# Two decoder layers on one core: ranks of eight experts on VectorE alone, and the order of the work made anew

## The chip, the cores and the metric

The kernel runs on one core of a Trainium2 chip. The metric is the device time in microseconds; lower is better. The core's engines work through queues of their own, each strictly in the order of the program: TensorE (PE, matmuls), VectorE (DVE), ScalarE (ACT), GpSimd (POOL), and SyncE (SP), which issues most transfers.

## The reference, cut to what matters

Sixteen sequences of 128 tokens with 256 features pass through two layers. Layer 0: causal attention, attention over a context with 16 heads, and a feed-forward net in which each token uses 4 of 16 blocks. Layer 1: self-attention, attention over the context in windows, and a mixture of eight experts:

```python
scores = jax.nn.sigmoid(x @ gate_weight.T)              # (tokens, 8)
topk_w, topk_idx = jax.lax.top_k(scores, 2)
topk_w = topk_w / (topk_w.sum(-1, keepdims=True) + 1e-20) * 2.5
combine = jnp.einsum('tk,tke->te', topk_w, jax.nn.one_hot(topk_idx, 8))
y = jnp.einsum('tei,ehi->teh', silu(g) * u, w_down)     # g, u: x by each expert's weights
out = jnp.einsum('te,teh->th', combine, y) + shared_out # an expert that all tokens use
```

Every step is preceded by a normalisation and added to its input. `top_k` breaks ties in favour of the lower index. The kernel gets the two largest by ranks: the rank of an expert is the number of experts with a larger score, plus the number of those with an equal score that come before it.

## The kernel before

The work is cut into eight lanes of two sequences (256 tokens). A lane's state `x0` to `x7` stays on chip from the first load to the last store. A lane is a chain of short steps that changes engine at almost every one: matmuls into one of four PSUM banks, copied or scaled by ScalarE or VectorE, sums and masks on VectorE, products and powers on GpSimd. One lane alone would leave TensorE idle most of the time, so several are interleaved.

The interleaving is made by a planner, the class `Turns`, while the program is being written out. Each step of a lane is a generator that yields the engine that it wants next, and the buffers that it takes (`yield DVE, dict(rank=2)`). `run` (line 229) picks, among all threads that wait, the one that can start first by the planner's own clock, and of equals the one with the lower rank; `charge` moves that clock. The order in which the steps are picked is the order of the instructions in every engine's queue, and nothing changes it later. The clock has constants: `PART` (added to TensorE at each turn, line 262), `RELEASE` (added to the time at which a buffer comes free, line 118), and in `indexed` (line 162) the time until an indirect transfer has landed.

`TURN` (line 1424) lists in which order the lanes begin layer 0 and layer 1; at most five are in flight. At the end of layer 1 the lanes part. Lanes 0 to 4 form a group: `routing` (line 954) ranks the experts and writes each token into a table sorted by expert; when all five are there, `plan` and 27 times `expert_tile` (line 1093) fetch one expert's weights and 128 tokens by two indirect transfers on GpSimd's queue, compute (`xgt`, `gu2`, `hT2`, `y2` on TensorE), and write the result `yo` back; `combining` (line 1145) then fetches four rows of results for each token of a lane, again by indirect transfers (`yg`), adds them to `x`, and stores it. `shared` (line 1011) is the expert that all tokens use. Lanes 5 to 7 run `expert_ffn` (line 1249) instead: all eight experts for every token, with weights that are zero for those not chosen. There a router's logits (`rt`) become scores (`sc`), the scores ranks, the ranks shares (`sel`), which are split into three parts of bfloat16 (`chosen`) and transposed by TensorE (`ptt`) before the experts' outputs can be weighted (`wb`).

`ranks` (line 636) is called for the 16 blocks of layer 0 (8 times) and for the eight experts of layer 1 (8 times). It makes two tensors of all pairs: `eq`, where another's score is equal, and `gt`, where it is larger. GpSimd multiplies `eq` by a triangle of ones and adds it to `gt`; VectorE sums over the others.

Of the kernel before, what the change touches and what calls it, by code (L numbers as in the profile page):

```python
# [9 lines left out]
F32 = mybir.dt.float32  # L10
I32 = mybir.dt.int32
BF16 = mybir.dt.bfloat16
U8 = mybir.dt.uint8
AF = mybir.ActivationFunctionType
ALU = mybir.AluOpType
AX = mybir.AxisListType

B, S, D = 16, 128, 256
P = 128
DC = D // P  # L20
G = 2
NL = B // G
# [9 lines left out]
NE, TOPE = 8, 2  # L32
# [42 lines left out]
PE, DVE, ACT, POOL, SP = "PE", "DVE", "ACT", "POOL", "SP"  # L75
# [6 lines left out]
class Turns:  # L82
# [7 lines left out]
    HOP = 70.0  # L90
    HOP_FROM_PE = 200.0
    SWITCH = 91.0
    PART = 0.0
    RELEASE = 0.0

    def __init__(self, nc, limits):
        self.nc = nc
# [64 lines left out]
    def indexed(self, out, out_index, src, src_index):  # L162

        at = lambda i: None if i is None else bass.IndirectOffsetOnAxis(ap=i, axis=0)
        self.charge(POOL, 1050.0)
        self.moved(4 * int(np.prod((src if src_index is None else out).shape)))
        self.now.at += 2000.0
        self.nc.gpsimd.indirect_dma_start(out, at(out_index), src, at(src_index))  # L168

    def fetch(self, out, src):  # L170
# [102 lines left out]
def decoder(ctx: ExitStack, tc: tile.TileContext, a: dict, out: bass.AP):  # L273
# [5 lines left out]
    small = ctx.enter_context(tc.tile_pool(name="small", bufs=4))  # L279
# [46 lines left out]
    def along(t, n):  # L326

        return t.unsqueeze(2).to_broadcast([t.shape[0], t.shape[1], n])
# [28 lines left out]
    class Sorted:  # L357
# [27 lines left out]
        rank=2, selT=2, p0=3, pT0=3, unseen=4, chosen=3, swap=1, words=1, top=3,  # L385
    )
    q = Turns(nc, LIMITS)

    def new(tag, shape, name, dtype=F32):
        return work.tile(shape, dtype, tag=tag, name=name, bufs=LIMITS[tag])  # L390
# [245 lines left out]
    def ranks(scores, n, tri_at):  # L636

        tri = consts[:, tri_at : tri_at + n * n].rearrange("p (e f) -> p e f", f=n)
        shape = [P, G, n, n]
        other = scores.unsqueeze(2).to_broadcast(shape)  # L640
        own = scores.unsqueeze(3).to_broadcast(shape)
        yield DVE, dict(rank=2)
        gt = new("rank", shape, "gt", BF16)
        eq = new("rank", shape, "eq", BF16)
        q.dve("tensor_tensor", eq, other, own, ALU.is_equal)
        q.dve("tensor_tensor", gt, other, own, ALU.is_gt)
        yield POOL
        q.pool("tensor_tensor", eq, eq, tri.unsqueeze(1).to_broadcast(shape), ALU.mult)
        q.pool("tensor_tensor", gt, gt, eq, ALU.add)
        yield DVE  # L650
        rank = small.tile([P, G, n], F32, tag=f"rank{n}", name="rank")
        q.dve("tensor_reduce", rank, gt, AX.X, ALU.add)
        q.give("rank", 2)
        return rank
# [594 lines left out]
    def expert_ffn(l):  # L1249
# [10 lines left out]
        rank = yield from ranks(sc, NE, C_TRI8)  # L1260
        sel = small.tile([P, G, NE], F32, tag="sel", name="sel")
        q.dve("scalar_tensor_tensor", sel, rank, float(TOPE), sc, ALU.is_lt, ALU.mult)
        den = small.tile([P, G], F32, tag="den", name="den")
        q.dve("tensor_reduce", den, sel, AX.X, ALU.add)
        q.dve("tensor_scalar", den, den, 1e-20, None, ALU.add)
        q.dve("reciprocal", den, den)
        q.dve("tensor_tensor", sel, sel, along(den, NE), ALU.mult)
        q.dve("tensor_scalar", sel, sel, 2.5, None, ALU.mult)
        yield DVE, dict(chosen=1)

        share = chosen.pop(0)
# [137 lines left out]
    def layer_1(l):  # L1409
        yield from self_attention(l)  # L1410
        yield from windowed_attention(l)
        ended.append((1, l))
        g = group_of.get(l)
        if g is not None:
            yield from routing(l)
            g.left -= 1
            at = q.now.at
            q.start(shared(l), 2 * NL + l + NL, at)
            if g.left == 0:
                q.start(sorted_experts(g), 2 * NL + min(g.lanes), at)  # L1420

    IN_FLIGHT = 5

    TURN = [(0, l) for l in range(6)]
    for l in range(NL):
        TURN += [(1, l), (0, l + 6)] if l + 6 < NL else [(1, l)]

    def more():
        n = begun[0]
# [119 lines left out]
```

## Time and profile before

| | |
|---|---|
| median of three timed runs | 829.65 us (828.49 to 832.1) |
| the profiled execution: own time | 827.16 us |
| its span, first to last instruction | 825.4 us |
| mean granted clock of TensorE | 0.985 |
| busy: PE, DVE, ACT, POOL | 777.8, 478.4, 393.0, 450.4 us |
| POOL, product eq<-eq and sum gt<-gt for eight experts | 488 and 425 ns, 8 times each |
| DVE, eq<-sc and gt<-sc | 291 and 284 ns, 8 times each |
| DVE, sum rank<-gt over 128 and over 512 elements | 278 and 676 ns, 8 times each |

A row of the profile names the line of the source, the engine, the operation, output and input tiles, their size in partitions by elements, how many instructions there were, and how long they took. Nearly all compute instructions have the line of a helper of `Turns` (L135 and L140 for TensorE, L144 VectorE, L149 ScalarE, L155 GpSimd, L168 indirect transfers), so the names of the tiles tell the steps apart. In rows in order of time the first two numbers are the start in us from the span's start and the time taken; the bracket at the end is how long the engine was idle before, and what it waited for. A matmul in float32 is two records. The 40 digits of a row of slices are tenths of busy time, or of full clock, in stretches of 20.6 us.

### The profile page before, as it was taken

The page shows a single profiled execution, that of the slowest core. Times are in us where ns is not written, and L with a number is a line of the kernel's source. Part 1 is how long each engine was busy: PE and PEld are TensorE (multiplying, and loading weights), DVE is VectorE, ACT ScalarE, POOL GpSimd, SP SyncE. Part 2 cuts the span into 40 slices and gives each one's busy share as a digit, 9 for nine tenths or more (in the row PEclk, how much of TensorE's full clock was granted, in tenths as well). Part 3 has the DMA queues.
Part 4 walks back from the last instruction along what each step waited for, and adds up shares of the span by engine and source line. Part 5 has one row for each costly group of instructions (what it writes and reads, how often), then busy time and mean ns, then how long its engine had stood idle before and what let it go on. Part 6 is the DMA issues. An engine that isn't in the chain of part 4 may idle for free.

```text
span 825.4 us, 19793 instructions
## 1 busy us (share of the span) xinstructions
PE 777.8 (94%) x7886; PEld 617.3 (75%) x7886; DVE 478.4 (58%) x1257; ACT 393.0 (48%) x874; POOL 450.4 (55%) x720
## 2 busy tenths in 40 slices
PE   6999999999999999999999999998997799999998
PEld 5777678878778777877777777776665677787776
DVE  4455736545735536746675668567765654434464
ACT  4546345343355364745663666575446244443300
POOL 5325535514335356656876747776675664654071
PEclk9999999999999999999999999999998899999999
DMA  8457540601201002020003301111110534455042
GB/s 292 154 155 217 147 141 25 185 17 36 58 2 40 14 30 62 2 65 15 15 20 100 126 27 39 63 56 40 50 56 15 178 94 133 153 185 160 26 133 84
DMA packets 60940, 70.41 MB, mean 85 GB/s; under 512 B 8848, under 2 KB 52496, under 8 KB 60208
## 3 DMA queue, kind: packets, MB, share of 16 engines
q1 hardware_dynamic: 51584, 46.20, 17.9%
q0 software_dynamic: 5376, 19.40, 7.7%
q10 hardware_dynamic: 3888, 3.54, 1.2%
q8 instruction: 62, 1.02, 0.5%
q14 instruction: 30, 0.25, 0.1%
HBM read 43.96 MB, written 20.97 MB: 79 GB/s over the span
## 4 chain that ended last, share of the span: by engine, by line
PE 77%; DVE 7%; POOL 6%; ACT 4%; issue 3%; DMA 1%; ACTq 0%; DVEq 0%; POOLq 0%
PE s L135 15%; PE pj L135 11%; PE y L135 11%; PE gu L135 10%; PE pr L135 9%; PE hp L135 8%; PE oT L135 4%; PE tps L140 3%; PE o L140 2%; ACT p L149 2%; DVE top L144 2%; POOL rstd L155 2%; PE rt L135 1%; POOL we L168 1%; POOL qs L155 1%
## 5 line engine op out<-in xcount | busy, mean ns | idle before, releaser
L144 DVE TENSOR_REDUCE top<-s 128x8 f32<-128x1024 f32 x96 | 113.0, 1218 | 53.7 <-PE s L135 50.0
L149 ACT ACTIVATE p<-s 128x1024 f32<-128x1024 f32 x96 | 95.1, 1024 | 63.1 <-PE s L135 61.6
L155 POOL TENSOR_TENSOR qs<-qT,less 128x512 f32<-128x512 f32 x48 | 61.8, 1293 | 66.2 <-ACT less L149 56.4
L135 PE MATMUL s<-qs,kb 32*128 32x128 f32 x1536 | 62.1, 288 | 7.3 <-POOL qs L155 3.1
L135 PEld LDWEIGHTS s<-qs,kb 32*128 32x128 f32 x1536 | 51.6, 189 | 22.6 <-issue 6.7
L155 POOL TENSOR_SCALAR rstd<-mv 128x2 f32<-128x2 f32 x77 | 18.5, 241 | 91.5 <-DVE mv L144 80.3
L135 PE MATMUL hp<-srcT,L_w 128*128 128x256 f32 x256 | 66.0, 387 | 0.0
L135 PE MATMUL s<-kb,qT 32*128 32x256 f32 x768 | 61.4, 405 | 4.3 <-DVE top L144 4.2
L149 ACT ACTIVATE sg<-gu 128x256 f32<-128x256 f32 (+1 forms) x67 | 22.9, 342 | 80.6 <-PE gu L135 78.7
L135 PE MATMUL y<-L_w,hm 128*128 128x256 f32 x256 | 58.8, 383 | 0.7 <-ACT gained L149 0.6
L155 POOL TENSOR_TENSOR rstd<-rstd,power 128x2 f32<-128x2 f32 x77 | 55.3, 718 | 6.4
L155 POOL TENSOR_SCALAR kb<-kT,consts 128x256 f32<-128x256 f32 x96 | 53.5, 568 | 6.9 <-ACT kT L149 6.0
L149 ACT ACTIVATE hm<-hp,cols 128x256 f32<-128x256 f32 x64 | 26.9, 471 | 59.1 <-PE hp L135 58.8
L135 PEld LDWEIGHTS s<-kb,qT 32*128 32x128 f32 x768 | 38.2, 184 | 21.2 <-issue 8.5
L135 PEld LDWEIGHTS y<-L_w,hm 128*128 128x128 f32 x256 | 47.7, 190 | 8.4 <-issue 1.1
L135 PE MATMUL oT<-p,v 128*32 128x128 f32 x1536 | 52.6, 278 | 0.8 <-ACT gained L149 0.5
L135 PEld LDWEIGHTS hp<-srcT,L_w 128*128 128x128 f32 x256 | 44.3, 190 | 11.6 <-issue 2.6
L144 DVE SCALAR_TENSOR_TENSOR sg<-sg,gu 128x256 f32<-128x256 f32 (+1 forms) x67 | 24.4, 364 | 43.6 <-ACT sg L149 43.3
L135 PE MATMUL gu<-srcT,gu 128*128 128x256 f32 x192 | 48.0, 399 | 1.3 <-DVE hm L144 0.7
L140 PE MATMUL tps<-consts,xn 128*128 128x128 f32 x244 | 38.4, 282 | 10.3 <-DVE xn L144 7.2
L135 PEld LDWEIGHTS oT<-p,v 128*32 128x32 f32 x1536 | 39.6, 111 | 11.0 <-issue 7.5
L168 POOL DMA_INDIRECT we<-in_L_experts,tile_weights x27 | 26.0, 965 | 39.6 <-PE hT L140 18.8
(211 smaller groups left out, 1796.7 us busy)
## 6 DMA issues: line engine op xcount, KB each, us to landing
to_experts<-zero SPq DMA_DIRECT2D x7, 1280.0 KB, 5.8
unseen<-hidden SPq DMA_DIRECT2D x128, 64.0 KB, 2.6
c<-in_ctx SPq DMA_DIRECT2D x16, 256.0 KB, 4.7
by_experts<-yo ACTq DMA_DIRECT2D x27, 128.0 KB, 1.9
x<-in_x SPq DMA_DIRECT2D x8, 256.0 KB, 6.6
L_w<-in_L_w SPq DMA_DIRECT2D x2, 1024.0 KB, 5.6
hidden<-plain SPq DMA_DIRECT2D x32, 64.0 KB, 1.6
swap<-kT SPq DMA_DIRECT2D x16, 128.0 KB, 2.0
```

Of the source, the lines that this page charges most:

```text
L135: self.nc.tensor.matmul(out, lhsT, rhs, **kw)
L140: self.nc.tensor.transpose(out, src, ident)
L144: getattr(self.nc.vector, name)(out, *args, **kw)
L149: getattr(self.nc.scalar, name)(out, *args, **kw)
L155: getattr(self.nc.gpsimd, name)(out, *args, **kw)
L168: self.nc.gpsimd.indirect_dma_start(out, at(out_index), src, at(src_index))
```

## The change

`ranks` has a branch of its own for the eight experts. One tensor holds both comparisons side by side, `equal` and `above`; the product with the triangle is made by VectorE in place, and one sum over both axes gives the ranks. GpSimd has no part in it any more, and the branch takes one buffer of the kind `rank` instead of two. In `expert_ffn` the shares are divided and scaled by 2.5 in one operation instead of two. The rest alters the planner: `PART` and `RELEASE` are 20 and 30 instead of 0, an indirect transfer is taken to land 1000 ns later, the shared expert of a lane has rank 16 + l instead of 24 + l, and seven lanes begin layer 0 before the first begins layer 1, instead of six. With these the planner picks another order for the whole program.

```diff
-    PART = 0.0
-    RELEASE = 0.0
+    PART = 20.0
+    RELEASE = 30.0
...
-        self.now.at += 2000.0
+        self.now.at += 3000.0
         self.nc.gpsimd.indirect_dma_start(out, at(out_index), src, at(src_index))
...
         other = scores.unsqueeze(2).to_broadcast(shape)
         own = scores.unsqueeze(3).to_broadcast(shape)
+        if n == NE:
+
+            yield DVE, dict(rank=1)
+            t = new("rank", [P, G, n, 2, n], "above", BF16)
+            above, equal = t[:, :, :, 0, :], t[:, :, :, 1, :]
+            q.dve("tensor_tensor", equal, other, own, ALU.is_equal)
+            q.dve("tensor_tensor", above, other, own, ALU.is_gt)
+            q.dve("tensor_tensor", equal, equal, tri.unsqueeze(1).to_broadcast(shape), ALU.mult)
+            rank = small.tile([P, G, n], F32, tag=f"rank{n}", name="rank")
+            q.dve("tensor_reduce", rank, t, AX.XY, ALU.add)
+            q.give("rank")
+            return rank
...
-        q.dve("tensor_tensor", sel, sel, along(den, NE), ALU.mult)
-        q.dve("tensor_scalar", sel, sel, 2.5, None, ALU.mult)
+        q.dve("scalar_tensor_tensor", sel, sel, 2.5, along(den, NE), ALU.mult, ALU.mult)
...
-            q.start(shared(l), 2 * NL + l + NL, at)
+            q.start(shared(l), 2 * NL + l, at)
...
-    TURN = [(0, l) for l in range(6)]
+    TURN = [(0, l) for l in range(7)]
     for l in range(NL):
-        TURN += [(1, l), (0, l + 6)] if l + 6 < NL else [(1, l)]
+        TURN += [(1, l), (0, l + 7)] if l + 7 < NL else [(1, l)]
```

## The prediction

> **What bounds the kernel now.** I read the engines' shares first, then the 40 slices, then the list of waits for TensorE alone, then the stretches of 25 us, and last the instructions in order of time at the places that these pointed to.
>
> ```profile
> PE 777.8 (94%) x7886; PEld 617.3 (75%) x7886; DVE 478.4 (58%) x1257; ACT 393.0 (48%) x874; POOL 450.4 (55%) x720
> PE   6999999999999999999999999998997799999998
> PEclk9999999999999999999999999999998899999999
> ```
>
> TensorE (PE) is busy 777.8 of 825.4 us, so 47.6 us idle. The slices are full until the 29th; the losses lie at the start, and from about 560 us on. By stretches the late ones look like this (columns: PE busy, weight loads, DVE, ACT, POOL, then the granted clock, the DMA share, GB/s):
>
> ```profile
> 600.00:625.00 25.00, 22.07 (x347) 15.61 (x344) 17.61 (x55) 12.05 (x24) 17.57 (x29) 0.93 0.14 39
> 625.00:650.00 25.00, 21.10 (x191) 17.38 (x192) 13.29 (x52) 15.00 (x30) 13.74 (x26) 0.86 0.22 70
> 650.00:675.00 25.00, 19.89 (x97) 15.98 (x100) 14.55 (x45) 6.79 (x21) 18.55 (x26) 0.86 0.39 116
> ```
>
> Here TensorE idles 2.9, 3.9 and 5.1 us, and its clock is down as well. The largest single wait is this one, a router's:
>
> ```profile
> 643.61 0.95 PE L135 MATMUL rt<-L_router,srcT 128*128 128x8 f32 x8
> 645.52 0.28 DVE L144 TENSOR_TENSOR gt<-sc 128x128 bf16<-128x128 f32 x1
> 652.26 0.56 POOL L155 TENSOR_TENSOR eq<-eq,consts 128x128 bf16<-128x128 bf16 x1
> 652.90 0.42 POOL L155 TENSOR_TENSOR gt<-gt,eq 128x128 bf16<-128x128 bf16 x1
> 653.56 0.25 DVE L144 TENSOR_REDUCE rank<-gt 128x16 f32<-128x128 bf16 x1
> 656.98 0.39 PE L135 MATMUL ptt<-ident,chosen 128*128 128x128 bf16 x2 [4.84 <-DVE chosen L144]
> ```
>
> VectorE (DVE) has both comparisons done at 645.80; GpSimd (POOL) takes up their product at 652.26, because five gathers of weights and a product of a rotation stand ahead of it in its queue. TensorE, in order, then waits 4.84 us at ptt. The same list gives ptt 6.3 us in two waits (the other 1.43, at 743.9).
>
> The end is read from the last 46 us:
>
> ```profile
> 779.60 0.59 PE L135 MATMUL y<-we,hT 128*128 128x256 f32 x2
> 784.82 0.94 POOL L168 DMA_INDIRECT yg<-by_experts,results  x1 [23.91 <-DVE results L144]
> 808.90 0.95 POOL L168 DMA_INDIRECT yg<-by_experts,results  x1 [0.30 <-issue]
> 812.32 0.48 DVE L144 SCALAR_TENSOR_TENSOR x<-yg,weight,x 128x256 f32<-128x256 f32 x1
> 820.53 1.03 PE L135 MATMUL y<-L_shared,hm 128*128 128x256 f32 x4
> 822.04 0.37 SPq L1317 DMA_DIRECT2D out_x<-x  x1
> ```
>
> Two things run side by side. From the last expert tile's y (779.60) the combining goes on alone: write back, 20 gathers at 1.25 us each on POOL, the last sum at 812.32-812.80. Meanwhile lane 7's dense experts keep TensorE busy to 821.4, and their output, issued at 822.04, ends the span. From an output's issue to the end are 825.4 - 822.04 = 3.4 us, so combining would end at 812.8 + 3.4 = 816.2: it has 9.2 us to spare. From the last tile's y it takes 816.2 - 779.6 = 36.6 us.
>
> **Part 1: ranks.** For the eight experts ranks are made 8 times. Per time, POOL loses 0.488 + 0.425 us (rows eq<-eq and gt<-gt, 128x128) and both hops. VectorE gains a product over the same 128 elements and sums 256 instead of 128. The product isn't in the trace on VectorE; eq<-sc with the same elements and two inputs takes 0.29 and is its nearest row; below it is bounded by the smallest VectorE rows, 0.16, above by POOL's 0.488. I take 0.29. The sum: 278 ns at 128 elements and 676 at 512, so 1.04 ns an element and 0.41 us at 256. VectorE: 8 x (0.29 + 0.13) = +3.4 us; POOL: -7.3. Scaling the shares in one operation replaces 0.17 + 0.23 by about 0.24, in three lanes: -0.5 us. None of this is on TensorE; the rest of VectorE's queue, 58% busy, covers it. Without that cover it would be 0.4 us for each router.
>
> A rule speaks against it: the Trainium skill, "SBUF — State Buffer" (section "Who interferes with whom"), says that a VectorE instruction with two SBUF inputs and a GpSimd instruction that reads SBUF shut each other out for a whole instruction. The row: eq and gt on sc have two SBUF inputs and take 0.28-0.29 in the seven routings that I read in the trace. By the rule, behind one POOL product of 1.29 us (qs) the new product could take 1.3 us more, 10 us over all eight on VectorE, three of them on a router's path. I go by the row and keep the rule for the upper end.
>
> On the path: in the wait above, from the start of rt to gt's end are 2.2 us, from rank to ptt 3.4. With product and longer sum between them instead of 7.8 us, rt to ptt is 2.2 + 0.3 + 3.4, the longer sum (0.13) about made up by the merged scaling: 5.9 instead of 13.4.
>
> **Part 2: the order.** The constants PART, RELEASE and the later landing of an indexed transfer only alter the planner's own clock; seven lanes of layer 0 ahead, and a shared expert's rank of 16 + l, alter what it picks. The program has the same matmuls and as many changes of tile shape (331 for 329), so TensorE's work is unchanged. ACT's and SP's queues carry the same operations and transfers, placed anew.
>
> (a) Behind the last expert tile's y there stood 44 gu, 40 y and 9 wb matmuls. Now there are 28, 20 and 7. Four 256-wide matmuls (8 records) take 1.73 us, so 36 x 0.433 + 2 x 0.1 = 15.8 us of work moved ahead of that tile. If nothing else changed, combining would end at 816.2 + 15.8 = 832.0, and TensorE (21.5 us plus an output's 4) would be done some 10 us sooner. So POOL's gathers set the end: +6.6 us, the 9.2 to spare being used up. The other side of this: the dense tail no longer counts, nor do its waits at 798-800.
>
> (b) Routers. In the new order between the starts of rt and ptt stand, for lane 5, the router's four, 8 gu, 2 y and 4 transposes: 0.81 + 3.46 + 0.87 + 0.45 = 5.6 us; for lane 6 5.2; for lane 7 over 40. Against 5.9 these are short by 0.3 and 0.7. So 6.26 us of waits become 1.0: -5.2.
>
> (c) The clock. After the 4.84 us gap the stretch 656-660 has a granted clock of 0.50, and 16 gu records take 4.76 us instead of 3.62. The rule of "TensorE: Matmul & The Clock Gate" (section "Part 1: The HAM clock gate") says half rate after an idle window of some 3.4 us. By it only this gap costs clock, 1.15 us. By the row it is more: in 637-641 the clock is 0.57 after gaps of only 1.71 and 0.90 us, and 8 pj records take 3.38 instead of 1.73. I go by the row: small gaps in a cluster count. For this gap: -1.15.
>
> (d) The last attentions. Between 590 and 640 us TensorE waits for qs, top, p, on: 0.2 + 1.8 + 0.5 + 0.8 + 0.4 + 0.8 + 1.3 + 0.3 + 1.7 + 0.9 = 8.7 us, and four groups at low clock cost some 3.7 more. In the old order the shared expert of lane 3 came after this and lane 4's behind the first expert tiles; in the new one those of lanes 1 to 4, 5.2 us of matmuls each, stand between these attentions. They can take in these gaps wholly (12.4) or not at all. I take the middle, -6.2.
>
> (e) The new order brings layer 1's lanes 0 and 1 closer together. Adding up POOL's rows as they are issued, some 33 us of them fall into one stretch of 25 us of matmuls after the middle; formerly the most was 25. VectorE gets 29 there. That can cost nothing (neighbouring stretches are light, 17 us) or up to the surplus, 6 us. I take 1.
>
> The sum: +6.6 - 5.2 - 1.15 - 6.2 + 1 = -4.95 us, a span of 820.4. The profiled execution's own time was 827.16 for its span of 825.4; the three timed runs have a median of 829.65, 2.5 above. I carry the difference over: 829.65 - 4.95 = 824.7.
>
> **Rivals.** (1) Slower: the end passes to the gathers, and the gains ahead don't come. For it: the 36.6 us behind the last tile are a chain of transfers that no order shortens, and the count of matmuls behind it is fixed. Against: the router's wait has a cause that the change removes. Place: POOL from the last tile on. With (b) and (c) lost to VectorE's queue or the port, nothing from (d): +6.6 + 1 = 837; it decides wherever less than 2.5 us is gained ahead of the last tile.
> (2) Only the routers gain; the last attentions keep their gaps, since each lane's chain of VectorE, ACT and POOL is no shorter: 6.6 - 6.35 + 1 = +1.25, 830.9. For it: the gaps' releasers are in-order engines, and filler on TensorE doesn't speed those.
> (3) The pile in (e) is paid in full beside rival 2: +6.3, 836. For it: POOL at 55% is uneven. Against: lanes in flight cover each other.
>
> **How the numbers follow.** My case has 0.45, rival 2 0.25, rivals 1 and 3 0.30 together. My own case runs from 817.5 (all of (d), no pile: -12.2) to 829. The range reaches from there, a little below, to the slower rivals with some of the port's price left out: 816 to 838. 0.5% is about what a measurement here can tell from no change, 4.1 us: under 825.5 is faster, over 833.8 slower. Of my case two thirds are under 825.5, with a little of rival 2: 0.36. Slower: rivals 1 and 3 but for a little, 0.31. The rest, 0.33, is no change.
>
> **What would show it.** (a): TensorE's last matmul some 5 to 10 us before the end, and the last output behind a yg sum. (b): ptt waits under 2 us, gt to rank about 1 us with nothing on POOL. (c), (d): clock of 1.00 and under 5 us idle in the stretches of the last attentions. (e): new waits of TensorE for qs, rstd or kb around 430 to 460 us. I'm wrong if TensorE is the last to end after all, or if the last tile's y comes later than 790 us.

## The result and the profile after

The changed kernel takes 841.55 us (median of four runs, 840.85 to 843.56) beside 830.88 us for the kernel before; the ratio is 1.0135, 95% interval 1.0102 to 1.0169. It is slower by about 11 us, where I had forecast 824.7 us and a range of 816 to 838 us. The profiled execution took 843.56 us, its span is 841.8 us, its mean granted clock 0.973.

The engines' shares and the 40 slices of the changed kernel (a slice is 21 us here):

```profile
PE 782.0 (93%) x7886; PEld 619.0 (74%) x7886; DVE 484.6 (58%) x1262; ACT 393.2 (47%) x874; POOL 443.6 (53%) x704
PE   6999999999999999999989799898988799999992
PEclk9999999999999999999999899998989799999997
```

TensorE is busy 4.2 us longer with the same matmuls, so the clock was lower. New thin slices stand in the middle (21st and 23rd), and the last slice is nearly empty of TensorE: its work ends well before the span does. Taking from the rows in order of time every stretch between the first and the last matmul in which none runs, TensorE idles 37.1 us in the kernel before and 37.1 us in the changed one. The waits have moved and not shrunk. Nearly all of the 16.4 us between the two spans are the 4.2 us of longer matmuls and 11.8 us behind TensorE's last matmul (15.6 us instead of 3.8). The medians are less far apart, 10.7 us, since the profiled execution of the kernel before was one of its quicker ones. Below, "waits" is this sum; of a single stretch, those over 0.25 us are added up.

The stretches of 25 us of the changed kernel (columns as in the prediction):

```profile
450.00:475.00 25.00, 19.56 (x217) 13.90 (x213) 22.18 (x53) 11.38 (x26) 20.79 (x36) 0.87 0.06 22
600.00:625.00 25.00, 22.98 (x263) 17.71 (x261) 20.51 (x60) 6.87 (x15) 11.44 (x20) 0.86 0.20 64
625.00:650.00 25.00, 22.37 (x198) 17.06 (x190) 15.16 (x34) 12.94 (x30) 17.17 (x28) 1.00 0.08 29
650.00:675.00 25.00, 19.81 (x246) 15.63 (x246) 19.73 (x60) 10.64 (x20) 15.75 (x23) 0.80 0.22 69
```

The first row was a full one before; now it lacks 5.4 us and has a clock of 0.87. The three others were 22.07, 21.10 and 19.89 before: 2.1 us fuller together, at a clock that is no better on the whole (0.93, 0.86 and 0.86 before). The waits in the middle, from the changed kernel's rows for TensorE in order of time:

```profile
441.79 1.10 PE L135 MATMUL pr<-L_qkv,srcT 128*128 128x256 f32 x4 [2.17 <-DVE on L144]
...
468.76 0.19 PE L135 MATMUL n<-sel,before 128*128 128x8 bf16 x2 [1.02 <-DVE sel L144]
...
471.40 1.98 PE L135 MATMUL s<-qs,kb 32*128 32x128 f32 x28 [2.37 <-POOL qs L155]
```

With six smaller ones they make 8.3 us between 437 and 473; the kernel before had none over 0.25 us there. Over the longer stretch from 400 to 540, TensorE idles 9.9 us instead of 4.3.

The router that waited 4.84 us at ptt now looks like this (all engines, in order of time):

```profile
661.57 0.96 PE L135 MATMUL rt<-L_router,srcT 128*128 128x8 f32 x8
...
662.11 1.41 POOL L155 TENSOR_TENSOR x<-x,rows 128x256 f32<-128x256 f32 x2
...
662.78 2.39 DVE L144 TENSOR_SCALAR sc<-sc 128x16 f32<-128x16 f32 x1 [0.29 <-ACT sc L149]
663.51 2.16 POOL L155 TENSOR_SCALAR kb<-kT,consts 128x256 f32<-128x256 f32 x4
...
665.94 0.28 DVE L144 TENSOR_TENSOR above<-above,consts 128x128 bf16<-128x128 bf16 x1
...
666.25 0.42 DVE L144 TENSOR_REDUCE rank<-above 128x16 f32<-128x256 bf16 x1
...
669.12 0.42 DVE L144 SCALAR_TENSOR_TENSOR hm<-sg,gu 128x256 f32<-128x256 f32 x1
...
669.69 2.05 PE L135 MATMUL y<-L_shared,hm 128*128 128x256 f32 x4 [3.60 <-DVE hm L144]
...
672.38 0.42 PE L135 MATMUL ptt<-ident,chosen 128*128 128x128 bf16 x2
```

Product and sum took 0.28 and 0.42 us, and ptt doesn't wait. But TensorE waits 3.60 us just ahead of it, for `hm` of a shared expert that stands behind the ranks in VectorE's queue. And `sc`, an operation on 16 elements that takes 0.17 us elsewhere, took 2.39.

The end:

```profile
803.08 0.59 PE L135 MATMUL y<-we,hT 128*128 128x256 f32 x2
808.33 0.95 POOL L168 DMA_INDIRECT yg<-by_experts,results  x1 [25.03 <-DVE results L144]
...
825.20 1.03 PE L135 MATMUL y<-L_shared,hm 128*128 128x256 f32 x4
...
830.69 5.47 SPq L1183 DMA_DIRECT2D out_x<-x  x2
...
832.27 0.95 POOL L168 DMA_INDIRECT yg<-by_experts,results  x1 [0.30 <-issue]
...
834.75 1.00 DVE L144 SCALAR_TENSOR_TENSOR x<-yg,weight,x 128x256 f32<-128x256 f32 x2 [0.91 <-DMA yg<-by_experts,results]
```

The last tile's y comes at 803.08 instead of 779.60. TensorE is done at 826.2; the twenty gathers go on to 833.2, the last sums to 835.8, and the last output ends the span at 841.8. From the last y to the end are 38.7 us (36.6 in my estimate).

### The profile page after: what moved, and what is told of

It reads as the page before. It is cut to its first block, busy times and chain, and to the rows that moved or that the text cites. A ratio compares the mean times of both kernels' runs of the same rounds, so it can differ in the third digit from the quotient of the medians.

```text
span 841.8 us, 19765 instructions
## 1 busy us (share of the span) xinstructions
PE 782.0 (93%) x7886; PEld 619.0 (74%) x7886; DVE 484.6 (58%) x1262; ACT 393.2 (47%) x874; POOL 443.6 (53%) x704
## 3 DMA queue, kind: packets, MB, share of 16 engines
q8 instruction: 62, 1.02, 0.5%
## 5 line engine op out<-in xcount | busy, mean ns | idle before, releaser
L135 PE MATMUL s<-qs,kb 32*128 32x128 f32 x1536 | 64.0, 298 | 10.9 <-POOL qs L155 5.7
L135 PEld LDWEIGHTS s<-qs,kb 32*128 32x128 f32 x1536 | 53.5, 198 | 24.1 <-POOL qs L155 9.5
L135 PE MATMUL s<-kb,qT 32*128 32x256 f32 x768 | 58.5, 401 | 0.6 <-DVE top L144 0.6
L140 PE MATMUL tps<-consts,xn 128*128 128x128 f32 x244 | 40.1, 288 | 10.4 <-DVE xn L144 8.3
L144 DVE TENSOR_TENSOR x<-x,y 128x256 f32<-128x256 f32 x32 | 13.4, 418 | 60.6 <-PE y L135 60.5
L135 PEld LDWEIGHTS s<-kb,qT 32*128 32x128 f32 x768 | 36.4, 184 | 16.0 <-issue 5.4
L135 PE MATMUL gu<-srcT,gu 128*128 128x256 f32 x192 | 45.9, 383 | 1.3 <-DVE hm L144 0.7
```

The source lines that it names most:

```text
L135: self.nc.tensor.matmul(out, lhsT, rhs, **kw)
L140: self.nc.tensor.transpose(out, src, ident)
L144: getattr(self.nc.vector, name)(out, *args, **kw)
```

## The experiments

All of them, with waits, clock and ends from each one's profile. Ratios are to the kernel before, timed beside them on the same chip, with 95% intervals.

| | ratio | waits, us | clock | last tile's y | TensorE's end | span |
|---|---|---|---|---|---|---|
| kernel before | 1 | 37.1 | 0.985 | 779.6 | 821.6 | 825.4 |
| changed kernel | 1.0135 (1.0102 to 1.0169) | 37.1 | 0.973 | 803.1 | 826.2 | 841.8 |
| 1 ranks alone | 0.9925 (0.990 to 0.995) | 36.2 | 0.983 | 778.6 | 820.7 | 824.5 |
| 2 order alone | 1.0189 (1.0154 to 1.0224) | 37.6 | 0.966 | 807.9 | 831.0 | 846.4 |
| 3 changed, no combining | 1.0002 (0.9981 to 1.0022) | 37.2 | 0.981 | 801.9 | 824.8 | 830.2 |
| 8 before, no combining | 0.9959 (0.994 to 0.9977) | 35.8 | 0.977 | 787.5 | 825.4 | 829.2 |
| 4 last dense lane late | 1.0114 (1.008 to 1.0148) | 45.8 | 0.975 | 795.2 | 835.9 | 839.7 |
| 5 dense work put back | 1.014 (1.0086 to 1.0194) | 44.6 | 0.979 | 794.9 | 835.4 | 839.2 |
| 6 ranks, old numbers | 0.9983 (0.996 to 1.0006) | 37.1 | 0.977 | 790.1 | 822.6 | 827.7 |
| 7 six lanes ahead | 1.0074 (1.0059 to 1.0089) | 37.3 | 0.976 | 795.2 | 829.0 | 834.7 |
| 9 ranks in one go | 0.9956 (0.9936 to 0.9975) | 36.5 | 0.986 | 778.8 | 820.2 | 824.0 |
| 10 gap at n filled | 1.0165 (1.011 to 1.0221) | 37.0 | 0.976 | 803.1 | 826.2 | 841.6 |
| 11 shared experts late | 1.0124 (1.0069 to 1.0178) | 37.7 | 0.977 | 801.0 | 824.2 | 839.5 |

The runs from 12 on were made where the kernel before itself took 847 us; they have a table of their own below.

**Ranks or order (1 and 2).** Run 1 keeps the old order on every engine (the planner is charged as before) and changes only the ranks and the scaling in one operation. Cut to what matters:

```diff
         yield POOL
-        q.pool("tensor_tensor", eq, eq, tri..., ALU.mult)
-        q.pool("tensor_tensor", gt, gt, eq, ALU.add)
+        q.charge(POOL, ...)            # as before, so that the order stays
+        nc.vector.tensor_tensor(equal, equal, tri..., ALU.mult)
+        q.charge(POOL, ...)
         yield DVE
-        q.dve("tensor_reduce", rank, gt, AX.X, ALU.add)
+        nc.vector.tensor_reduce(rank, t, AX.XY, ALU.add)
```

> The kernel before with its own order, every engine's instructions where they stood, and only the ranks of the eight experts (product on VectorE, one sum over both comparisons) and the one-operation scaling changed. Theory A (the order is what costs): TensorE's waits at ptt, 6.3 us in the kernel before, go to under 1.5 us, the low clock behind them goes with them, and the time falls by 3 to 8 us, ratio 0.990 to 0.996. Rival B (the ranks on VectorE cost by themselves, through VectorE's queue or the lock between VectorE and GpSimd): the time rises by 3 us or more, ratio 1.004 or above, with new waits of TensorE behind VectorE at the routers. Rival C (the end hides it: gathers and dense experts have slack of 9 us, dense work is the last): within 2 us of before.

Run 2 keeps the new order and makes the ranks of the eight on GpSimd as before:

```diff
-            q.dve("tensor_tensor", equal, equal, tri..., ALU.mult)
-            q.dve("tensor_reduce", rank, t, AX.XY, ALU.add)
+            nc.gpsimd.tensor_tensor(eq, eq, tri..., ALU.mult)
+            nc.gpsimd.tensor_tensor(gt, gt, eq, ALU.add)
+            nc.vector.tensor_reduce(rank, gt, AX.X, ALU.add)
```

> The changed kernel with its own order, and only the ranks of the eight experts made as before: product and sum on GpSimd. Theory A: the order alone is as slow as the whole change or slower, ratio to the kernel before 1.012 to 1.025; the waits at ptt come back only in part, since dense work stands between router and ptt in the new order. Rival B (ranks on VectorE are the cost): the time falls back towards before, ratio 0.997 to 1.006.

Both verdicts go to theory A. The ranks gain 0.75% in the old order (1 to 0.9925) and 0.5% in the new one (1.0189 to 1.0135, though these two intervals overlap); the order costs 1.9% to 2.1% whichever way the ranks are made. Run 1 is faster than both kernels of this case. But my mechanism for its gain is not confirmed. Run 1's rows at the router that waited 4.84 us:

```profile
653.49 1.61 DVE L144 TENSOR_TENSOR swap<-swap,consts 128x512 f32<-128x512 f32 x1
655.02 0.28 DVE L651 TENSOR_TENSOR above<-above,consts 128x128 bf16<-128x128 bf16 x1
...
659.25 0.39 PE L135 MATMUL ptt<-ident,chosen 128*128 128x128 bf16 x2 [5.27 <-DVE chosen L144]
```

The product is on VectorE and ptt still waits 5.27 us, because the product now stands behind other work in VectorE's queue in place of GpSimd's. What is gone are the waits behind it, between 680 and 790: 0.7 us of them instead of 3.9 (the second router's ptt, 1.4, and one of an expert tile's gu, 1.6). In this pair of profiles 2.2 us more of waits between 540 and 680 took most of that back. Run 2 says the same of the new order: with the ranks still on GpSimd TensorE waits only 0.5 us at ptt there, and 2.31 us at `y<-hm` just ahead of it. So it was the order, and not the ranks, that took the waits away from ptt.

**Is it the end? (3 and 8.)** The gathers of combining and the sums behind them are left out, the order kept:

```diff
         def one(j, k):
             yield POOL
-            q.indexed(y[:, i, :], None, g.by_experts, by[:, i : i + 1])
+            q.charge(POOL, 1050.0)     # and the rest of indexed's charges
             yield DVE
-            q.dve("scalar_tensor_tensor", x..., y..., weight..., x..., ALU.mult, ALU.add)
+            q.charge(DVE, 150 + 1.05 * D)
```

In the changed kernel:

> The changed kernel without the gathers of combining and their sums: the routed experts of the lanes that are sorted are left out of the output; all other work and its order are kept. Theory A (combining sets the end): TensorE's last matmul ends where it did, near 826 us, and the span ends some 4 to 6 us after it, 830 to 832 instead of 841.8: 10 to 12 us less than the whole change, ratio to before 0.998 to 1.003. Rival (the end is set by TensorE, or the gathers only take time that an output's landing needs anyway): less than 4 us less, ratio 1.009 or above.

The end of run 3, all engines in order of time:

```profile
823.76 1.03 PE L135 MATMUL y<-L_shared,hm 128*128 128x256 f32 x4
...
824.83 0.42 DVE L144 TENSOR_TENSOR x<-x,y 128x256 f32<-128x256 f32 x1 [3.90 <-PE y L135]
825.27 0.37 SPq L1327 DMA_DIRECT2D out_x<-x  x1
825.69 1.01 SPq L1182 DMA_DIRECT2D out_x<-x  x2
```

TensorE's last matmul releases the last outputs again; the ratio falls from 1.0135 to 1.0002, by 1.33% or 11 us. The same in the kernel before:

> The kernel before, its order kept, without the gathers of combining and their sums: the routed experts of the sorted lanes are left out of the output. Theory A (in the kernel before combining is hidden behind the dense experts): within 0.3% of before, TensorE the last to end as before. Rival (gathers disturb TensorE through memory traffic or GpSimd's share of the ports): faster by 0.5% or more.

Here leaving it out brings 0.41%, 3.4 us, a little more than theory A allowed: combining was not quite hidden. The two waits at 798 and 800 (1.48 and 0.51 us, for `hm`) are absent in run 8; sums that waited for gathers had stood ahead of `hm` in VectorE's queue, as these rows of the kernel before show:

```profile
798.29 0.48 DVE L144 SCALAR_TENSOR_TENSOR x<-yg,weight,x 128x256 f32<-128x256 f32 x1 [3.12 <-DMA yg<-by_experts,results]
...
799.16 0.27 PE L135 MATMUL wb<-selT,experts 128*128 128x256 bf16 x1 [1.48 <-DVE hm L144]
```

So combining costs 3.4 us in the old order and 11.0 in the new one. Of the 11.2 us that the change costs (1.35% of 830.9), 7.6 are its end, and 3.6 (1.0002 less 0.9959; the intervals allow some 2 us either way) were lost ahead of it.

**Can the end be had back? (4 and 5.)** Run 4 lets the last dense lane begin only when all tiles have been put in order; run 5 lets its router go ahead, and holds back only what follows it, and the output matmuls of the lane before:

```diff
-        if ready and experts_begun[0] < len(dense):
+        if ready and experts_begun[0] < len(dense) and (experts_begun[0] < 2 or tiles_done):   # run 4
...
-        yield PE, dict(hm=5)                                                                  # run 5
+        yield PE, (dict(hm=5, gate=1) if l == NL - 1 else dict(hm=5))
...
         yield [expert_tile(g, i) for i in range(g.tiles)]
+        q.give("gate", 2)
```

> The changed kernel in which the last dense lane's experts may begin only when all expert tiles have been put in order, so that its matmuls stand behind the last tile again; planner and all else as changed. Theory A: the last tile's y comes 12 to 18 us earlier, TensorE is again the last to end, and of the 11.7 us of change 8 to 11 go: ratio 1.000 to 1.005; the gaps at 440 to 470 us and at the last attentions stay as in the changed kernel. Rival (tiles wait for their weights or for TensorE's own lateness, not for the dense work ahead): the last tile's y comes at most 4 us earlier, ratio 1.010 or above.

> The changed kernel with its order up to the last expert tiles; only, the seventh lane's dense output matmuls and the eighth lane's dense experts after its router (its eight experts and shared expert) may begin once all expert tiles have been put in order. Some 14 us of TensorE's work go back behind the last tile; routers stand where they did. Theory A (the moved dense work is why the end is set by gathers): the last tile's y at 787 to 792 us instead of 803.1, TensorE again the last to end, near 826 to 829, span 830 to 833, ratio 0.998 to 1.005. Rival (the last tiles are late for reasons of their own, weights or gathers of rows): last y after 797 us and ratio above 1.008.

Neither theory had this right. In both the last tile comes about 8 us earlier and TensorE is the last to end, as theory A said; and both are as slow as the changed kernel. In run 4 the lane's router was held back with it and waits 4.33 us at ptt with nothing beside it. Run 5 has no such fault. Its expert tiles, in TensorE's rows:

```profile
783.69 0.30 PE L140 MATMUL hT<-consts,h 128*128 128x128 f32 x1 [0.67 <-DVE h L144]
...
787.01 0.30 PE L140 MATMUL hT<-consts,h 128*128 128x128 f32 x1 [0.88 <-DVE h L144]
...
792.06 1.13 PE L135 MATMUL gu<-we,xgT 128*128 128x256 f32 x4 [1.07 <-ACT xgT L149]
794.20 0.33 PE L140 MATMUL hT<-consts,h 128*128 128x128 f32 x1 [1.01 <-DVE h L144]
```

A tile is a chain from TensorE to ScalarE, VectorE and back. With fewer dense matmuls between its links TensorE waits at them: from 680 us on the waits are 10.6 us instead of 2.4 in the changed kernel, 6.3 of them between 777 and 795. The dense work that the new order moved ahead was in use there as cover. It can cover the tiles or the gathers; that the new order has not enough of it left for both is my reading of these two runs. In the old order TensorE waited only 3.9 us between 680 and 790 with this work behind the last tile; what covered the tiles there was not traced.

**Which of the planner's numbers? (6, 7, 11.)** Run 6: all five as before, ranks as changed and charged as changed. Run 7: only the lanes ahead. Run 11: only the shared expert's rank.

```diff
-    TURN = [(0, l) for l in range(7)]                 # runs 6 and 7
+    TURN = [(0, l) for l in range(6)]                 # and l + 6 in the loop
...
-            q.start(shared(l), 2 * NL + l, at)        # runs 6 and 11
+            q.start(shared(l), 2 * NL + l + NL, at)
```

> The ranks and the scaling as in the changed kernel and charged as there, all five numbers of the planner (six lanes ahead, shared expert's rank 24 + l, part 0, release 0, 2000 after an indexed transfer) as before; the order follows from that. Theory A (the five numbers bring the loss): ratio 0.985 to 0.998, no new waits at 440 to 470 us, ptt waits under 2 us. Rival (any order made anew loses against the old one, since the numbers of the kernel before were picked for it): ratio 1.005 or above. By the count of matmuls 6 us fewer stand behind the last tile than in the kernel before, so that the gathers would end about level with TensorE.

> The changed kernel with six lanes of layer 0 ahead again in place of seven, all else as changed; order made anew. Theory A (seven lanes ahead bring layer 1's first lanes together and make the new waits at 439 to 472 us, 8.3 us in the changed kernel): there under 4 us, clock back to 0.978 or above; behind the last tile 5.6 us more matmuls than in the changed kernel, so the end gains that too: ratio 0.998 to 1.006. Rival (the waits come from the planner's other numbers): the waits stay above 6 us, ratio 1.008 or above.

> The changed kernel with the shared expert's rank of 24 + l again, all else as changed; order made anew. Theory A (shared experts between the last attentions fill nothing there, and used up cover that the expert tiles want later): waits at 540 to 680 us within 2 us of the changed kernel's 16.6, time the same or up to 4 us less, ratio 1.008 to 1.014; the last tile's y as late as in the changed kernel, since by the count as little work stands behind it. Rival (they do fill, as I forecast with 6.2 us): waits at 540 to 680 us grow by 3 to 8 us and the time with them, ratio 1.016 or above.

Run 7: the waits between 437 and 473 fall from 8.3 to 2.9 us, and the time by 0.6%, 5 us. But the one doesn't explain the other. Between 400 and 540 TensorE idles 9.5 us, as in the changed kernel (9.9), so the waits only left the narrow stretch. What differs is the end: the last tile's y comes at 795.2 instead of 803.1, and 5.7 us instead of 15.6 stand behind TensorE's last matmul. The forecast ratio of at most 1.006 was missed by a little; a router at the end now waits 3.49 us.

Run 11: 0.1% in time, within the intervals, and waits of 17.4 us between 540 and 680 instead of 16.6. It does not test what it was made for. By the tiles' names TensorE's order is that of the changed kernel up to 653 us, and the shared experts stand where they stood. A row of the changed kernel, and the same in run 11:

```profile
617.98 3.62 PE L135 MATMUL gu<-srcT,L_shared 128*128 128x256 f32 x8
```

```profile
616.07 3.62 PE L135 MATMUL gu<-srcT,L_shared 128*128 128x256 f32 x8
```

So it is not their rank that put them between the last attentions, and whether they fill anything there stays untested.

Run 6 comes out just above theory A's ratio. Ranks and scaling are those of the changed kernel, so the five numbers together cost 1.5% (0.9983 to 1.0135). With the old numbers and only the charges of the ranks different, the order changes so that the first router stands behind the plan's 20 small operations in VectorE's queue. ptt itself waits 0.64 us, but just ahead of it TensorE waits 9.88 us for the same `chosen`:

```profile
660.66 1.40 PE L140 MATMUL ot<-consts,xn 128*128 128x128 f32 x4 [9.88 <-DVE chosen L144]
```

Its waits still sum to 37.1 us.

**Is a wait worth its length? (9.)** The old order on TensorE, ScalarE and GpSimd, with product, sum and choice directly behind the comparisons in VectorE's queue (in the five routings for the sorted table, product and sum only):

```diff
             q.dve("tensor_tensor", above, other, own, ALU.is_gt)
+            nc.vector.tensor_tensor(equal, equal, tri..., ALU.mult)
+            nc.vector.tensor_reduce(rank, t, AX.XY, ALU.add)
+            if then:
+                then(rank)            # sel, den, the scaling, chosen
             yield POOL
```

> The kernel before with its order on TensorE, ACT, GpSimd and SyncE; ranks of the eight on VectorE as in the first experiment, but here product and sum follow the two comparisons at once in VectorE's queue, and in the three unsorted lanes the choice too, up to what ptt reads. Theory A (the ranks help where VectorE takes them up at once, the order decides that): the wait of 5.27 us at ptt that was left in the first experiment goes to under 1 us, the time is 2 to 6 us below that experiment's 825.9, ratio to before 0.985 to 0.991. Rival (the next chain takes up what is gained, since the waits before ptt grow when TensorE comes sooner): ptt falls, other waits grow by as much, ratio 0.990 to 0.995. Rival B (VectorE's other work, held up 2.5 us by the choice, is late for TensorE): ratio above 0.995.

TensorE's rows of run 9, from ptt on:

```profile
649.11 0.28 PE L135 MATMUL ptt<-ident,chosen 128*128 128x128 bf16 x2
...
658.02 0.41 PE L140 MATMUL xgt<-consts,we 128*128 128x128 f32 x2 [0.59 <-DMA we<-to_experts,tile_rows]
...
659.76 0.41 PE L140 MATMUL xgt<-consts,we 128*128 128x128 f32 x2 [1.32 <-DMA we<-to_experts,tile_rows]
...
661.29 0.60 PE L140 MATMUL xgt<-consts,we 128*128 128x128 f32 x2 [1.12 <-DMA we<-to_experts,tile_rows]
...
665.70 0.69 PE L140 MATMUL xgt<-consts,we 128*128 128x128 f32 x2 [3.82 <-ACT xgT L149]
```

By its mechanism the rival is right. No router waits any more, and new waits stand at the first expert tiles: 3.03 us for their rows, and 3.82 us for ScalarE, which was held up itself:

```profile
664.79 0.60 ACT L149 ACTIVATE xn<-x,less,rstd 128x256 f32<-128x256 f32 x1 [8.77 <-POOL less L155]
```

Both lead to GpSimd's queue: it issues the gathers of these rows from 654.54 on, in the kernel before from 654.69 on, and `less` stands behind them. They come no sooner, so the 4.84 us were slack of this next chain. The ratio, 0.9956, lies just outside the rival's range and inside rival B's, so the time alone would not tell the two apart.

**Does a gap lower the clock? (10 and 12.)** Matmuls on constants fill a gap, 44 before the fourth lane's n in the changed kernel, 80 before the sixth lane's ptt in the kernel before:

```diff
+            for _ in range(44):
+                nc.tensor.matmul(wide[:, GT : GT + P], before, ident16, start=True, stop=True)
             for j in range(G):
                 q.matmul(n[:, j, :], before, sel[:, j, :], start=True, stop=j == 0)
```

> The changed kernel with 44 matmuls on constants (128 columns, bf16, result read by nothing) in front of the fourth lane's matmul n, at which TensorE waits 2.97 us. Theory A (such a gap halves the clock of the next 4 to 6 us): with the gap filled the granted clock in the 12 us from the gap's start on is 0.95 or above instead of 0.76, 0.50 and 0.89, TensorE is busy some 3 us longer for the filling and some 2.5 us less for the rest, and the matmuls after n take 1.2 instead of 2.1 us; the time falls by up to 3 us. Rival (the clock falls by itself there, for power or for lack of matmuls over a longer stretch, and the gap doesn't cause it): the clock stays at 0.5 to 0.9 and the time the same or more.

Run 10 could not tell. The filling itself waited 2.98 us, so what n had waited for was its PSUM bank, held until VectorE's sum on `x`:

```profile
572.84 4.85 PE L1002 MATMUL n<-ident,before 128*128 128x128 bf16 x44 [2.98 <-DVE x L144]
```

It took 110 ns for each matmul, half speed right behind the gap.

> The kernel before with 80 matmuls on constants (128 columns, bf16, result read by nothing) in front of the sixth lane's ptt, where TensorE waits 4.84 us for VectorE's choice; at full clock they take some 4.4 us. Theory A (the gap lowers the clock that follows): the wait at ptt shrinks to under 1 us and the granted clock in the 4 to 8 us after it is 0.95 or above instead of 0.50; the 16 gu records behind it take 3.6 instead of 4.76 us; the time is the same to 0.3% less, since the first tiles' rows come no sooner. Rival (the clock falls for another reason, by load over a longer time): the clock behind ptt is 0.5 to 0.7 as before.

Run 12's row for the filling, then two stretches of 4 us behind it; below them the same stretches of the kernel before (columns as above, the clock third from the end):

```profile
657.02 4.63 PE L661 MATMUL ptt<-ident,before 128*128 128x128 bf16 x80
```

```profile
656.00:660.00 4.00, 4.00 (x60) 3.78 (x59) 3.73 (x15) 0.00 (x0) 3.75 (x5) 1.00 0.45 157
660.00:664.00 4.00, 3.85 (x42) 3.43 (x40) 1.36 (x7) 0.00 (x0) 3.03 (x4) 1.00 0.77 213
```

```profile
656.00:660.00 4.00, 3.02 (x9) 2.48 (x10) 1.34 (x6) 0.37 (x1) 3.09 (x4) 0.50 0.76 207
660.00:664.00 4.00, 4.00 (x18) 3.33 (x17) 0.96 (x3) 0.61 (x2) 3.51 (x5) 0.84 0.65 158
```

Filled at 58 ns a matmul the gap costs no clock: 1.00 where there were 0.50 and 0.84. (In run 17, the kernel before where it takes 847 us as in run 12, the same two stretches have 0.50 and 0.50.) The gap is the cause. But the other half of theory A failed. The 16 gu records behind the filling were to take 3.6 us and took 5.73 from the first's start to the last's end, since TensorE idles four times among them, 1.18 us together, and the releaser is no engine:

```profile
664.92 1.11 PE L135 MATMUL gu<-srcT,gu 128*128 128x256 f32 x4 [0.40 <-issue]
```

No row says why. The ratio, 0.9991 (0.9977 to 1.0005), allows for a gain of up to 1.9 us, so it can't tell whether the clock's 1.15 us were gained.

**The last two numbers (13 to 16), and two controls (17, 18).** Part and release undone, and the landing of an indexed transfer undone, each alone:

```diff
-    PART = 20.0
-    RELEASE = 30.0
+    PART = 0.0                       # runs 13 and 15
+    RELEASE = 0.0
...
-        self.now.at += 3000.0
+        self.now.at += 2000.0        # runs 14 and 16
```

> The changed kernel with part and release of the planner's clock at zero again, all else as changed; order made anew. By the count of matmuls the first expert tile stands 22 us earlier on TensorE than in the changed kernel, and 43.5 us of work stand behind the last tile instead of 21.9. Theory A (these two numbers make the last tile late and with it the loss): last tile's y at 776 to 790 us, TensorE the last to end, ratio 0.990 to 1.004. Rival (with dense work kept for the end the tiles lack cover, as when it was held back by hand): waits in the tiles' stretch of 5 us or more above the kernel before, ratio 1.008 or above.

> The changed kernel with an indexed transfer counted as landing 2000 again, all else as changed; order made anew. By the count of matmuls 28.3 us stand behind the last tile instead of 21.9. Theory A (the end follows from how much stands behind the last tile): the gathers end the span about 5 us earlier than in the changed kernel, ratio 1.004 to 1.010. Rival (what is moved behind is lacking as cover for the tiles): ratio 1.011 or above.

> The changed kernel with part and release of the planner's clock at zero, once more, on another chip. Theory A (these two numbers make the last tile late and with it the loss): last tile's y at 776 to 795 us, TensorE the last to end, ratio 0.990 to 1.004. Rival (with dense work kept for the end the tiles lack cover, as when it was held back by hand; in the run before TensorE waited 4.5, 2.5, 2.9 and 1.5 us at the first tiles, ahead of the disturbed stretch): waits between 640 and 790 us of 15 us or more, ratio 1.008 to 1.025.

> The changed kernel with an indexed transfer counted as landing 2000, once more, on another chip. Theory A (the end follows from how much stands behind the last tile): gathers end the span about 5 us earlier than in the changed kernel, ratio 1.004 to 1.010. Rival (a router without cover behind the last tile, a wait at ptt of 7.9 us in the run before, takes back what the later dense work gives): ratio 1.011 to 1.018.

> The kernel before, unchanged. Ratio 1.000, within 0.3%. If its clock is near 0.98, as in most of its executions, its profile should show waits of some 37 us in sum as in the first one, and 3 to 5 us more of busy time at a lower clock.

> The first experiment once more. Theory A (the ranks on VectorE gain 3 to 6 us): ratio 0.991 to 0.996; the waits' sum within 2 us of the kernel before, the rest by the clock. Rival (the gain was chance): ratio 0.998 to 1.002.

| | ratio | waits, us | of these 540 to 790 | from 790 on | last tile's y |
|---|---|---|---|---|---|
| 17 kernel before | 1.0011 (0.9996 to 1.0026) | 52.7 | 24.6 | 13.3 | 786.8 |
| 18 ranks alone | 0.9971 (0.9957 to 0.9985) | 50.1 | 21.8 | 13.3 | 784.4 |
| 12 before, ptt filled | 0.9991 (0.9977 to 1.0005) | 48.7 | 20.1 | 13.3 | 787.4 |
| 13 part, release undone | 1.0338 (1.0307 to 1.0369) | 65.2 | 30.9 | 14.7 | 812.4 |
| 15 the same again | 1.0344 (1.0307 to 1.038) | 67.4 | 32.3 | 14.6 | 810.8 |
| 14 landing undone | 1.0171 (1.0138 to 1.0204) | 62.9 | 25.0 | 19.9 | 803.4 |
| 16 the same again | 1.0186 (1.0134 to 1.0238) | 60.5 | 24.6 | 19.0 | 800.0 |

In these runs everything took some 16 us longer, of which 11 lie at the end: the kernel before has 13.3 us of waits from 790 on instead of 2.0. Its rows there:

```profile
815.34 0.38 ACT L149 ACTIVATE sg<-gu 128x256 f32<-128x256 f32 x1 [10.92 <-remote]
...
816.69 0.37 PE L135 MATMUL wb<-selT,experts 128*128 128x256 bf16 x1 [7.61 <-issue]
```

No row names a cause for it, and I leave it open; run 17's forecast of some 37 us of waits was missed by it. Ratios hold only within the group, and the changed kernel itself was not timed there, so its 1.0135 can be set beside these ratios only with care. Theory A fails for both numbers. The changed kernel with part and release undone is 3.4% slower than the kernel before, with waits of 31 to 32 us between 540 and 790 instead of 24.6; TensorE is also busy 14 to 18 us longer, at clocks of 0.957 and 0.960. With the landing undone it is 1.7% to 1.9% slower, with a wait of 7.9 us at a router's ptt behind the last tile, where nothing covers it (the rivals' reasons). So no single number, undone alone, takes the loss away; the lanes ahead come nearest (1.0074). Part and release apart, or pairs of numbers, were not tried. Run 18 repeats run 1: faster again, by 0.3%, which lies between the two forecast ranges; its interval leaves out 1.

## Why the prediction was wrong

The sum was +6.6 - 5.2 - 1.15 - 6.2 + 1 = -4.95 us, and by the ratio the change cost 11.2. By place: the end was to cost 6.6 and cost 7.6; everything ahead of it was to gain 11.55 and cost 3.6. By part of the change: the ranks, (b) and (c), were to gain 6.35 and gained 4.5 to 6.2 (runs 2 and 1); the order, (a), (d) and (e), was to cost 1.4 and cost 15.7 (1.89% of 832 us, run 2). The step that failed, in (b) and (d) alike, is to count a wait of TensorE at its length: single waits went, and the sum stayed at 37.1 us. Beside it (e) was too small, and no term had the 4.2 us by which TensorE is busy longer. Term by term:

**Part 1 held in its sizes and missed a cost.** Product 0.28 us (I took 0.29), sum 0.42 (0.41). VectorE was to gain 2.9 us and gained 6.2. The rest is in operations that last longer, `sc<-sc` above all: 1.4 us for eight before, 5.1 after. I had looked for the port's price at the product, which never paid it in this kernel (278 to 288 ns); in runs 1 and 18 one of the eight took 1.17 us. The Trainium skill, "SBUF — State Buffer", section "Who interferes with whom", counts tensor_scalar among the operations that can take both ports and then block against GpSimd for a whole instruction, and I had used only the part on two inputs. That `sc` is slow while GpSimd works agrees with it; that its 2.39 us span four of GpSimd's operations is more than one instruction, and no run isolates the cause. That rt to ptt takes 5.9 us was wrong too: from rt at 661.57 to the last `chosen` at 671.75 are 10.2, with 2.39 for `sc` and another lane's statistics and gate ahead of `chosen`.

**(b), -5.2: the ptt waits went, the time did not go with them.** They fell from 6.3 to 0.3 us, by the order (run 2). A wait of 3.60 us at `y<-hm` took the place of the largest, which was my open question about VectorE's queue, and run 9 shows more: with no new wait at the router, the next chain takes it up. The failed step is "So 6.26 us of waits become 1.0: -5.2". It takes a wait's length for its worth, with no look at what the next matmuls need. That the ranks alone gain 0.3% to 0.75% comes near the sum of (b) and (c) by luck: in run 1 it came with the first wait still in place.

**(c), -1.15: right about the chip, its worth not measured.** Run 12 shows gap and clock as cause and effect; a gain of 1.15 us is too small for its interval. In the changed kernel as many us of waits stand in other clusters, and TensorE is busy 4.2 us longer. Not all of that is the change's: where the kernel before takes 831 us it has clocks from 0.975 to 0.990 over its executions, and the profiled one, with 0.985, was one of the quicker; the changed kernel has 0.973 to 0.975.

**(d), -6.2: not there.** Waits between 540 and 680 are 16.4 us before and 16.6 after. Without the router's 4.84 before, and without the 2.97 at n and the 3.60 at `y<-hm` that are new, 11.5 and 10.0 are left: at most 1.5 us went. The failed step is "I take the middle": nothing in the profile said what part of a gap a filler takes. Rival 2's reason, that each lane's chain through the other engines sets the pace and "filler on TensorE doesn't speed those", fits the releasers (qs, top, on), but no run shows it, since run 11 left the shared experts in place.

**(e), +1: the size was off.** It came where it was forecast, 437 to 473, with releasers qs, sel and on. Between 400 and 540 TensorE idles 5.6 us more than before (9.9 instead of 4.3), where I took 1 and had 6 as the upper end, as in rival 3. What these waits cost in time no run isolates; run 7 keeps nearly all of them and gains its 5 us elsewhere.

**(a), +6.6: right in kind, and 1 us small.** The gathers set the end, and runs 3 and 8 give 7.6 us for it. But TensorE is done 15.6 us before the end, where I expected 5 to 10, and one of my own signs of being wrong came true: the last tile's y is later than 790 us. The 15.8 us moved ahead of it would have put it at 795.4; it came at 803.1, since ahead of it time was lost too. I also counted the 15.8 us as merely moved. In run 5, which holds such work back, the tiles wait for lack of cover, so that moving it back doesn't undo the loss.

Rival 1 described what happened: the end passes to the gathers and the gains ahead don't come. Its 837 used the low price for (e). With rival 3's price for (e), +6.6 + 6 = +12.6 or 842.25 us, it would have been within 1 us of the 841.55 measured, in part by luck: the end cost 7.6 and all ahead of it 3.6. The range stopped at 838 because I treated the two as alternatives that share 0.30, though nothing in the profile made them exclude each other.

## What to carry to other kernels

Before counting a wait as a gain, ask what the waiting engine needs next and when that is ready: here eleven of the thirteen kernels in the first table kept 35.8 to 37.7 us of waits, with different orders and single waits removed, while their times ran from 0.9925 to 1.0189. (The two that held dense work back have 44.6 and 45.8 us.) Independent work that fills gaps is a stock; moving it earlier takes it from the place where it covered something, so say for each piece what it covered before and what covers that now. And a change of an operation should be tried with the order held fixed before the order is made anew: the operation gained here, and the new order took back more than twice that.

## What the hardware showed that I had not expected

- A VectorE operation on 16 elements lasted through four of GpSimd's: `sc<-sc`, 0.17 us at best, took 2.39 while GpSimd ran `x<-x,rows` (0.73 us) and three of the four `kb` (0.54 us each). Over eight of them the mean is 175 ns before, 634 after, and 360 in run 2, which has the same order and the ranks on GpSimd.
- A gap of 2.98 us was followed by matmuls at half speed at once (110 ns for a 128-column bf16 matmul, 58 ns at full clock), for some 6 us. The Trainium skill, "TensorE: Matmul & The Clock Gate", section "Part 1: The HAM clock gate", has half rate after an idle window of some 3.4 us; here less was enough. Length alone doesn't decide: in the changed kernel the gap of 2.17 us at 441.79, with 0.68 us behind it, left the clock at 1.00 (stretch 425 to 450).
- The same 37.1 us of waits went with 777.8 and with 782.0 us of busy time, at clocks of 0.985 and 0.973: a sum of waits doesn't tell what they do to the clock. In the changed kernel the stretch 450 to 475, with waits of 1.02 and 2.37 us close together, has 0.87.
- The kernel before takes some 831 us on the chips of runs 1 to 11 and 847 on those of runs 12 to 18, with 11 us of the difference in waits of the combining stretch. The second group was also timed later, so that the chip is not shown to be the cause.
